# Cross attention in seven-product form on one core: half of the values' partition-group moves go from ScalarE to VectorE, and the values' sums stand ahead of the first transfer for x

## The chip, the cores and the metric

One core of one Trainium2 chip runs the kernel. The time is device microseconds of one execution, and the figure for a kernel is the median of its runs. The profile comes from one further execution, whose span (first to last instruction) is a little shorter than its device time.

## The reference, cut to what matters

x and y (`ctx_2048`) have the shape (32, 256, 1024): 32 samples, 256 channels C, 1024 positions N. Everything is fp32.

```
x_q = einsum('oc,bcn->bno', w_qk, y)
x_k = einsum('oc,bcn->bon', w_qk, x)
x_v = einsum('oc,bcn->bon', w_v, x) + b_v[None, :, None]
energy = einsum('bnc,bcm->bnm', x_q, x_k)
attention = softmax(energy, axis=-1)
attention = attention / (1e-07 + attention.sum(axis=1, keepdims=True))
x_r = einsum('bcn,bnm->bcm', x_v, attention)
x_r = relu(einsum('oc,bcn->bon', w_t, x - x_r) + b_t[None, :, None])
return x + x_r
```

Each row of the attention is normalized over m, then each column over n. The output is x plus a ReLU of a projection of x minus the attended values.

## The kernel before, in words

The weights are folded once: keys use w_qk^T w_qk, values use w_t w_v. After that the kernel loops over 32 samples b. Every matrix product is done in a 2x2 block form with seven products instead of eight (class `Seven`, methods `p1` to `p7`), so operands need sums of blocks (tiles `xs`, `ys`, `gt`, `us`, `et`), and the outputs are combined from PSUM banks (`c11`, `c12`, `c21`, `c22`). ScalarE copies products 1 and 5 and a partial result `w` out of PSUM (`kept`; tiles named `ep1s`, `ep5s`, `ew` for the energy), because later products are accumulated onto the same banks: product 6 goes onto bank one only after `ep1s` is copied, product 7 onto it only after `ew`, product 3 onto bank two only after `ep5s`.

For a sample there are four families of products: the keys (`Keys`, PSUM tiles `pg`, 7 products), the values (`Values`, `pu`, 7), the energy (`Energy`, `pe`, four row pairs t = 0 to 3, 28 products) and the attention with its projection (`Attention`, `po`, 35 products: 7 of x, 28 of the attention). That is 77 products of 128x128 by 128x512 for each sample. The trace records each as two MATMUL instructions.

The stages overlap by hand. The engines' instructions are issued in the order of the program (wrapper `InOrder`), and every engine works through its own queue in that order. The keys and values of sample b+1 and the first products of its energy are put among the energy and attention products of sample b. The loop over t runs the energy: `p1`, `p5`, `p6`, `p2`, `p3`, `p7` for t = 0; for later t, `p4` of the row pair before stands between `p6` and `p3`. Each pair's exponentials are on ScalarE (`exp`), the combining reductions with a running minimum or maximum and the column sums (`share`) on VectorE. Afterwards `columns` and `inverse` normalize the columns, and `Attention.run` scales e (`normal`), forms the sums `et` (`mix`) and multiplies.

The part that is changed: the values of the next sample come out with channels on the partitions and are needed with positions on the partitions. `Values.turn` transposes 32x32 blocks on VectorE from `ut` into `turned` (four instructions of 128x512), and `Values.move` then carries the blocks from one group of 32 partitions to another, back into `ut`. There are sixteen moves of 32 partitions x 512 elements, one for each pair of source and target group. Before the change all sixteen are ScalarE copies, in three lots in the energy of sample b at t = 0 (lines 669 to 719): six ahead of `p1`, four behind `p5`, six at the end of t = 0. (For the first sample they are DMAs on SyncE's queue.) When they are done, GpSimd forms the four sums `us` of the values (`Values.factors`), which the attention of that sample needs.

`summed("x", b + 1)` issues two plain loads from SyncE's queue into `xs` and returns three accumulating transfers, which GpSimd's queue issues (`xsteps`): each one waits for the one before it to land. Before the change the first stands at the end of t = 0, ahead of the four `us` sums, and the other two at the ends of t = 2 and t = 3.

Of the kernel before, what the change touches and what calls it, by code (L numbers as in the profile page):

```python
# [16 lines left out]
def kernel(  # L17
# [30 lines left out]
    B, C, N = x.shape  # L48
# [33 lines left out]
    pe, dve, act, pool = (InOrder(g) for g in (nc.tensor, nc.vector, nc.scalar, nc.gpsimd))  # L82
# [6 lines left out]
    def load(tag, b, pieces=1):  # L89
        from_, p = (x, xp) if tag == "x" else (y, yp)  # L90
        to = p.tile([P, KC, N], F32, tag=tag, name=f"{tag}_{b}")
        from_ = from_[b].rearrange("(k p) n -> p k n", p=P)
        W = KC // pieces
        for j in range(pieces):
            nc.sync.dma_start(to[:, ts(j, W)], from_[:, ts(j, W)])
        loaded[tag, b] = to

    def quarters(from_):

        return from_.rearrange("(k p) (h n) -> p k h n", p=P, h=MH)  # L100

    def corners(from_):

        q = quarters(from_)[:, 0, 0, :]
        return bass.AP(
            tensor=q.tensor, offset=q.offset, ap=[q.ap[0], [P * N + MB, 2], q.ap[-1]]
        )

    def accumulate(into, from_):
        return pool.dma_start(into, from_, accum_op=ALU.add)  # L110
# [113 lines left out]
    def summed(tag, b):  # L224


        p = up if tag == "x" else one
        s = p.tile([P, 4, MB], F32, tag=f"{tag}s", name=f"{tag}s_{b}")
        t1, t3, t4, t2 = (s[:, j] for j in range(4))
        to = loaded[tag, b]  # L230
        b11, b12 = to[:, 0, ts(0, MB)], to[:, 0, ts(1, MB)]
        b21, b22 = to[:, 1, ts(0, MB)], to[:, 1, ts(1, MB)]
        if b == 0:
            pool.tensor_tensor(t1, b11, b12, ALU.add)
            pool.tensor_tensor(t2, b22, t1, ALU.add)
            pool.tensor_tensor(t3, b12, b22, ALU.add)
            pool.tensor_tensor(t4, b21, t2, ALU.add)
            steps = []
        else:
            from_ = (x if tag == "x" else y)[b]  # L240
            q = quarters(from_)
            nc.sync.dma_start(s[:, :2], q[:, 0, 1:2, :].to_broadcast([P, 2, MB]))
            nc.sync.dma_start(s[:, 2:], q[:, 1])
            steps = [
                lambda: accumulate(s[:, :2], corners(from_)),
                lambda: accumulate(s[:, 2:], s[:, 0:1].to_broadcast([P, 2, MB])),
                lambda: accumulate(t4, q[:, 1, 1]),
            ]
        return (b11, b21, b22, t4, t1, t2, t3), steps
# [345 lines left out]
    def columns(b):  # L595

        dve.tensor_reduce(
            parts[:, :, 0],
            acc.rearrange("p (j r) -> p j r", r=G32),
            AX.X,  # L600
            ALU.add,
            apply_transpose=True,
        )
# [5 lines left out]
    def inverse(b):  # L609


        sc = one.tile([P, NB, 1], F32, tag="sc", name=f"sc_{b}")
        s = sc[:, :, 0]
        for a in range(1, NG):
            moved(parts[:G32, :, a], parts[ts(a, G32), :, 0])
        dve.tensor_reduce(s[:G32], parts[:G32], AX.X, ALU.add)
        dve.reciprocal(s[:G32], s[:G32])
        moved(s[G32 : 2 * G32], s[:G32])
        moved(s[2 * G32 :], s[: 2 * G32])
        rc = one.tile([P, NB, G32], F32, tag="rc", name=f"rc_{b}")  # L620
        dve.transpose(rc.rearrange("p j r -> p (j r)"), sc.to_broadcast([P, NB, G32]))
        return rc.rearrange("p j r -> p (j r)")
# [25 lines left out]
    xn, xsteps = summed("x", 1)  # L648
    xsteps[0]()
    u = Values(0, xr)  # L650
# [11 lines left out]
    for b in range(B):  # L662
        more = b + 1 < B
        pair = []

        for t in range(HT):
            now = Energy(b, t, lhs, rhs)
            pair.append(now)
            if t == 0 and b > 0:
                u.move(6, act.copy)  # L670
            now.p1()
            if t > 0:
                pair[t - 1].exp(1)
            now.p5()
            if t == 0:
                if b == 0:
                    u.p4()
                    u.c21()
                    u.turn()
                    u.move(16, nc.sync.dma_start)  # L680
                    xsteps[1]()
                    xsteps[2]()
                else:
                    u.move(4, act.copy)
                if b > 0 and more:
                    before.end()
                    before.c21()
                    load("x", b + 1)
                e = ep.tile([P, NT, N], F32, tag="e", name=f"e_{b}")
                acc = one.tile([P, N], F32, tag="acc", name=f"acc_{b}")  # L690
                if before is not None:

                    pool.tensor_copy(behind, before.t4[:, HT - 1, :1])
                for step in gsteps:
                    step()
            if t > 1:
                pair[t - 2].share(0)
            if t == 0:
                now.p6()
            now.p2()  # L700
            now.c11()
            if t == 1:
                pair[0].scale(1)
            if t > 1:
                pair[t - 1].share(1)
            if t > 0:
                now.p6()
            if t == 1:
                act.activation(acc, e[:, HT, :], AF.Copy, scale=scales[HT])
            if t > 0:  # L710
                pair[t - 1].p4()
                pair[t - 1].c21()
                pair[t - 1].exp(0)
            now.p3()
            now.c12()
            now.p7()
            now.c22()
            if t == 0:
                u.move(6, act.copy)
                ur, usteps = u.factors()  # L720
                if more and b > 0:
                    xn, xsteps = summed("x", b + 1)
                    xsteps[0]()
                for step in usteps:
                    step()
            elif more and b > 0 and t > 1:
                xsteps[t - 1]()
        last = pair[-1]

        if more:  # L730
            g = Keys(b + 1, xn)
            g.p1()
        last.exp(1)
        if more:
            g.p5()
        else:
            before.xpart(before.one, 7, True)
        pair[2].share(0)
        last.p4()
        last.c21()  # L740
        last.share(1)
        if more:
            load("y", b + 1)
            rhs, ysteps = summed("y", b + 1)
            g.p6()
        else:
            before.epart(before.one, 7)
        last.exp(0)
        if more:
            g.p2()  # L750
            g.c11()
            g.p3()
        else:
            now = Attention(b, xr, ur)
            now.begin()
        last.share(0)
        columns(b)
        if more:
            g.p7()
            g.c12()  # L760
            g.c22()
            un = Values(b + 1, xn)
            un.p1()
            un.p5()
            un.p2()
            un.p6()
        else:
            before.c22()
        rc = inverse(b)
        if more:  # L770
            un.p3()
            g.p4()
            g.c21()
            un.p7()
            lhs, gsteps = g.factors()

        if more:
            now = Attention(b, xr, ur)
            now.begin()
            ysteps[0]()  # L780
            now.run(un)
            if b + 2 < B:
                now.xpart(now.one, 7, True)
                now.epart(now.one, 7)
                now.c22()
                now.put()
            now.put()
            ysteps[1]()
            ysteps[2]()
            before = now  # L790
            xr, u = xn, un
        else:
            before.end()
            now.run(None, before)
            now.finish()
# [30 lines left out]
```

## Time and profile before

| | us |
|---|---|
| median of three runs | 2181.16 (2179.96 to 2182.82) |
| the profiled execution's device time | 2179.43 |
| its span | 2177.7 |
| PE busy in it | 2145.1 (99%) |
| DVE (VectorE) busy | 1793.1 (82%) |
| ACT (ScalarE) busy | 1096.0 (50%) |
| POOL (GpSimd) busy | 540.0 (25%) |
| granted TensorE clock | 0.998 |

Starts are microseconds from the start of the span. A line of the timeline gives start, length, engine, operation, target and source tile, shapes and how many instructions are merged into it, and in brackets how long the engine was idle before it and who ended that. Successive matmuls and successive VectorE instructions overlap at their ends, so the pitch from start to start is shorter than the length shown. Nearly all instructions carry line 77, which is the line of the recording wrapper; tiles tell them apart.

### The profile page before, as it was taken

The numbers are of one execution on the slowest core, as the hardware profiler recorded it, in microseconds if no ns is written. First come the engines' busy times: TensorE is split into PE (matmuls) and PEld (weight loads), VectorE is DVE, ScalarE is ACT, GpSimd is POOL, SyncE is SP. The second block draws the span as 40 slices with busy tenths as digits, with TensorE's granted clock in tenths as the row PEclk, the third lists the DMA queues.
The fourth block names the chain that finished last, engine by engine and source line by source line (L and its number), as shares of the span: only waits on it lengthen the run. The fifth ranks groups of instructions, "written<-read, shape, count | busy, mean of one in ns | idle before, by whom it ended". The sixth has DMA issues, their size and how long they took to land.

```text
span 2177.7 us, 17656 instructions
## 1 busy us (share of the span) xinstructions
PE 2145.1 (99%) x4972; PEld 933.7 (43%) x4972; DVE 1793.1 (82%) x3247; ACT 1096.0 (50%) x1818; POOL 540.0 (25%) x487
## 2 busy tenths in 40 slices
PE   9999999999999999999999999999999999999989
PEld 5444444444444444444444444444444444444433
DVE  6889778897778987788977889778897778987778
ACT  5444564445554455544455444564445654355542
POOL 4312222222222122221222312222222222222220
PEclk9999999999999999999999999999999999999999
DMA  6444544435444454444444444544435444354420
GB/s 174 102 107 110 135 126 106 121 92 140 122 112 125 95 127 130 121 111 106 116 128 133 102 104 113 135 126 107 117 96 140 122 108 128 92 130 128 119 54 29
DMA packets 114210, 249.94 MB, mean 115 GB/s; under 512 B 17088, under 2 KB 17856, under 8 KB 114112
## 3 DMA queue, kind: packets, MB, share of 16 engines
q0 software_dynamic: 42656, 81.28, 23.1%
q1 hardware_dynamic: 71456, 167.53, 21.9%
q8 instruction: 40, 0.66, 0.1%
q14 instruction: 58, 0.48, 0.1%
HBM read 181.67 MB, written 33.55 MB: 99 GB/s over the span
## 4 chain that ended last, share of the span: by engine, by line
PE 69%; ACT 17%; DVE 11%; issue 2%; ACTq 0%; DVEq 0%
PE po L77 27%; PE pe L77 24%; ACT ut L77 14%; PE pg L77 9%; PE pu L77 9%; DVE et L77 4%; DVE turned L77 3%; DVE e L77 1%; DVE z L77 1%; ACT z L77 1%; ACT ep1s L77 1%; ACT ep5s L77 1%; ACT ew L77 1%; DVE acc L77 0%; PE idle L77 0%
## 5 line engine op out<-in xcount | busy, mean ns | idle before, releaser
L77 PE MATMUL pe<-gt,ys 128*128 128x512 f32 x768 | 398.7, 601 | 26.4 <-ACT ep1s L77 18.8
L77 ACT COPY ut<-turned 32x512 f32<-32x512 f32 x496 | 305.3, 615 | 164.5 <-DVE turned L77 158.3
L77 DVE SCALAR_TENSOR_TENSOR e<-e,ri,rc 128x512 f32<-128x512 f32 x512 | 347.4, 747 | 1.1
L77 PE MATMUL po<-et,us 128*128 128x512 f32 x768 | 347.5, 594 | 0.7 <-DVE et L77 0.7
L77 DVE SCALAR_TENSOR_TENSOR acc<-e,ri,acc 128x1024 f32<-128x1024 f32 x224 | 288.3, 1287 | 8.0
L77 PE MATMUL pe<-gx,y 128*128 128x512 f32 x512 | 261.9, 593 | 0.0
L77 PEld LDWEIGHTS pe<-gt,ys 128*128 128x128 f32 x768 | 141.0, 190 | 230.9 <-issue 178.6
L77 PE MATMUL po<-e,ut 128*128 128x512 f32 x512 | 224.9, 592 | 0.0
L77 PEld LDWEIGHTS po<-et,us 128*128 128x128 f32 x768 | 143.2, 190 | 189.4 <-issue 145.8
L77 ACT ACTIVATE e<-e,nm 128x1024 f32<-128x1024 f32 x128 | 146.9, 1148 | 97.0 <-DVE nm L77 96.1
L77 POOL TENSOR_TENSOR gt<-gx 128x512 f32<-128x512 f32 x64 | 80.9, 1264 | 433.7 <-DVE gx L77 433.7
L77 DVE TENSOR_TENSOR z<-z,x 128x512 f32<-128x512 f32 x31 | 21.5, 692 | 182.8 <-ACT z L77 182.8
L77 POOL DMA_DIRECT2D xs<-in_x_dram x62 | 65.8, 1061 | 363.2 <-PE pe L77 225.9
L77 DVE TENSOR_TENSOR et<-e 128x1024 f32<-128x1024 f32 x128 | 153.7, 1222 | 2.3
L77 DVE CUSTOM_DVE_ANT_0 e<-pe,ep1s 128x512 f32<-128x512 f32 x128 | 88.2, 689 | 79.4 <-ACT ep1s L77 57.4
L77 PEld LDWEIGHTS pe<-gx,y 128*128 128x128 f32 x512 | 97.6, 191 | 123.0 <-issue 122.5
L77 PEld LDWEIGHTS po<-e,ut 128*128 128x128 f32 x512 | 97.3, 190 | 122.5 <-issue 99.0
L77 ACT ACTIVATE e<-e,bias 128x1024 f32<-128x1024 f32 x128 | 147.4, 1151 | 1.4 <-DVE bias L77 0.5
L77 PE MATMUL pe<-gt,y 128*128 128x512 f32 x256 | 131.3, 595 | 0.0
L77 PE MATMUL pe<-gx,ys 128*128 128x512 f32 x256 | 130.8, 592 | 0.2 <-DVE nm L77 0.2
L77 ACT ACTIVATE op5s<-po,bt 128x512 f32<-128x512 f32 x32 | 22.0, 687 | 200.5 <-PE po L77 200.5
L77 ACT ACTIVATE op1s<-po,bt 128x512 f32<-128x512 f32 x32 | 22.0, 687 | 197.7 <-PE po L77 197.7
(117 smaller groups left out, 3315.5 us busy)
## 6 DMA issues: line engine op xcount, KB each, us to landing
y<-in_ctx_dram SPq DMA_DIRECT2D x32, 1024.0 KB, 4.9
out_dram<-z SPq DMA_DIRECT2D x128, 256.0 KB, 2.1
x<-in_x_dram SPq DMA_DIRECT2D x31, 1024.0 KB, 7.5
xs<-in_x_dram SPq DMA_DIRECT2D x62, 512.0 KB, 4.6
ys<-in_ctx_dram SPq DMA_DIRECT2D x62, 512.0 KB, 4.5
xs<-in_x_dram POOLq DMA_DIRECT2D x31, 512.0 KB, 6.2
xs<-xs POOLq DMA_DIRECT2D x31, 512.0 KB, 5.0
ys<-in_ctx_dram POOLq DMA_DIRECT2D x31, 512.0 KB, 6.2
```

The source lines that it names most:

```text
L77: self.last = getattr(self.engine, name)(*args, **kwargs)
```

## The change

Of the sixteen moves of a sample, the first eight are now VectorE copies, issued right behind the last `put` of the sample before (for the last sample the first twelve). The remaining eight stay on ScalarE: five ahead of `p1` of t = 0 and three behind `p5`; the lot at the end of t = 0 is gone. For the last sample, ScalarE does four, at the end of t = 0, and none ahead of that. The four `us` sums on GpSimd now stand in t = 0 behind the sums of the keys (`gsteps`), and the three accumulating transfers for x come after them, at the ends of t = 1, 2 and 3. The two plain loads for `xs` keep their place in SyncE's queue.

```diff
             now = Energy(b, t, lhs, rhs)
             pair.append(now)
-            if t == 0 and b > 0:
-                u.move(6, act.copy)
+            if t == 0 and b > 0 and more:
+                u.move(5, act.copy)
             now.p1()
...
                     xsteps[1]()
                     xsteps[2]()
-                else:
-                    u.move(4, act.copy)
-                if b > 0 and more:
+                elif more:
+                    u.move(3, act.copy)
                     before.end()
                     before.c21()
                     load("x", b + 1)
...
                 for step in gsteps:
                     step()
+                if more:
+                    ur, usteps = u.factors()
+                    for step in usteps:
+                        step()
...
             now.c22()
-            if t == 0:
-                u.move(6, act.copy)
+            if t == 0 and not more:
+                u.move(4, act.copy)
                 ur, usteps = u.factors()
-                if more and b > 0:
-                    xn, xsteps = summed("x", b + 1)
-                    xsteps[0]()
                 for step in usteps:
                     step()
-            elif more and b > 0 and t > 1:
+            elif t == 0 and b > 0:
+                xn, xsteps = summed("x", b + 1)
+            elif more and b > 0:
                 xsteps[t - 1]()
...
             now.put()
+            un.move(8 if b + 2 < B else 12, dve.tensor_copy)
             ysteps[1]()
             ysteps[2]()
```

The prediction calls a product by its number and row pair: "p6 of t = 1" is the sixth product of the energy's second row pair.

## The prediction

> **What bounds the kernel now.** First the page's busy times. TensorE is busy for 2145.1 of 2177.7 us, VectorE for 82% of them; no other engine is near.
>
> ```profile
> PE 2145.1 (99%) x4972; PEld 933.7 (43%) x4972; DVE 1793.1 (82%) x3247; ACT 1096.0 (50%) x1818; POOL 540.0 (25%) x487
> ```
>
> So the question is how far TensorE is from running without a gap. In the PE timeline, fifteen undisturbed products from 638.47 to 651.35 give a pitch of 12.88 / 15 = 0.859 us. A sample has 77 products, 66.1 us. Samples start (p1 of t = 0) at 622.72, 690.01, 757.30: 67.29 us. TensorE loses 1.17 us a sample, about 35 us over the kernel, and that is all there is to gain between the two ends. The PE timeline shows where they lie:
>
> ```profile
> 630.44 1.02 PE L77 MATMUL pe<-gt,y 128*128 128x512 f32 x2
> 631.49 1.10 PE L77 MATMUL pe<-gt,ys 128*128 128x512 f32 x2
> 632.42 1.02 PE L77 MATMUL pe<-gx,y 128*128 128x512 f32 x2
> ...
> 634.14 1.02 PE L77 MATMUL pe<-gx,y 128*128 128x512 f32 x2
> 635.77 1.12 PE L77 MATMUL pe<-gt,ys 128*128 128x512 f32 x2 [0.61 <-ACT ep1s L77]
> 636.73 1.02 PE L77 MATMUL pe<-gx,ys 128*128 128x512 f32 x2
> ```
>
> Read start to start against 0.86. The line at 631.49 is p7 of t = 0 and comes 1.05 after its neighbour, 0.19 late; the next is 0.07 late. The line at 635.77 is p6 of t = 1 and comes 1.63 after its neighbour, 0.77 late, the next 0.10. Together 1.13 us. Another 0.04 is in the attention, where a product waits for the second half of an `et` sum. These lines return in every sample from 1 to 30 within 0.02 us.
>
> Who makes them late is in the ACT timeline:
>
> ```profile
> 622.78 3.76 ACT L77 COPY ut<-turned 32x512 f32<-32x512 f32 x6 [5.12 <-DVE turned L77]
> ...
> 627.66 2.50 ACT L77 COPY ut<-turned 32x512 f32<-32x512 f32 x4
> 630.18 0.69 ACT L77 ACTIVATE z<-po,bt 128x512 f32<-128x512 f32 x1
> 630.76 0.58 ACT L77 COPY ew<-pe 128x512 f32<-128x512 f32 x1
> 631.37 3.74 ACT L77 COPY ut<-turned 32x512 f32<-32x512 f32 x6
> 635.13 0.58 ACT L77 COPY ep1s<-pe 128x512 f32<-128x512 f32 x1
> ```
>
> ScalarE works through sixteen moves at 0.625 us with no idle time from 622.78 on. `ew` ends at 631.34 and holds p7; `ep1s` of t = 1 ends at 635.71 and holds p6, though its product (p1, 632.42) was through at 633.4.
>
> At the same time VectorE has nothing to do:
>
> ```profile
> 623.52 1.28 DVE L77 SCALAR_TENSOR_TENSOR z<-z,x 128x512 f32<-128x512 f32 x2
> 630.90 0.69 DVE L77 TENSOR_TENSOR z<-z,x 128x512 f32<-128x512 f32 x1 [6.09 <-ACT z L77]
> 631.51 0.68 DVE L77 CUSTOM_DVE_ANT_0 e<-pe,ep1s 128x512 f32<-128x512 f32 x1
> ```
>
> The moves go into that idle stretch of 6.09 us, 624.8 to 630.9.
>
> **The change part by part.**
>
> *ScalarE.* Eight moves go: 8 x 0.625 = 5.0 us. Its queue becomes: five moves from 622.78 to 625.90, `ep1s` and `ep5s` of t = 0 to 627.0, three moves to 628.9. The last attention product ends at 628.9, so `z` runs from 628.95 to 629.6. p6 of t = 0 ends at 629.74 (its start 628.72 plus 1.02), so `ew` runs from 629.8 to 630.4: p7, which TensorE could take at 631.30, no longer waits. Then ScalarE stands idle until p1 of t = 1 is through at about 633.2, `ep1s` is done at 633.8, and p6 is due at 634.73: 0.9 us to spare. All four late products go, the 0.07 and 0.10 with them, since they only follow an interrupted stream.
>
> *VectorE.* Eight copies of 32x512 are added. No copy of that kind is in the trace of before. The nearest rows of VectorE at 512 elements a partition are these:
>
> ```profile
> L77 DVE TENSOR_TENSOR z<-z,x 128x512 f32<-128x512 f32 x31 | 21.5, 692 | 182.8 <-ACT z L77 182.8
> L77 DVE MEMSET zeros<- 128x512 f32 x1 | 0.5, 485 | 0.1
> ```
>
> By the two-input row a move costs 0.69 us, eight 5.5, ending at 630.3. The Trainium skill ("VectorE: DVE Perf Modes", the perf-mode tier table) says that an fp32 copy inside SBUF runs at two elements a cycle, where a tensor_tensor has only one: by it and its 0.96 GHz, 256 cycles fewer than the row, 0.69 - 0.27 = 0.42 us (an estimate), and eight 3.4. I take 0.43, near the single-source memset row, and keep 0.42 to 0.69. The choice hardly matters in samples 1 to 30, as both ends lie under the cover of 6.09 us. What is queued behind the moves: the `z` addition (now possible at 629.7), then `c11`, `c12`, `c22` and `bias` of t = 0. Counting back from p3 of t = 1, due at 636.45: it needs `ep5s`, which stands behind the first exponential (1.15) on ScalarE, which needs `bias`; so `c22` must start by 633.75, and the moves must end by about 631.7. That is 6.9 us for eight, 0.86 each.
>
> *GpSimd and the transfers.* The four `us` sums (1.27 us each) start when the last move is done, about 629.0, and end at about 634.1; before, 635.2 to 640.3. The first accumulating transfer for x moves from 629.75 to about 634.1, the second from 640.22 to about 642.4, the third from 645.52 to about 648.5 (8.3 and 6.1 us from issue to next issue, as at 24.29, 32.57 and 38.71 in the first sample). Their readers are the next keys: product 5 at 652.2, product 6 at 653.9, product 4 at 661.6, each some 1.1 us earlier after the change. The second lands at about 649, four microseconds ahead of product 6; the third, at 4.0 us to landing plus about 1 of issue, at about 653.5, seven ahead of product 4. Cost nothing; if that cover were gone, lateness would hit TensorE directly. The plain loads on SyncE keep their place, so no other transfer is passed.
>
> A rule that speaks against this: the Trainium skill ("SBUF — State Buffer", "Who interferes with whom") says that a VectorE copy using both ports locks GpSimd out for its whole length, descriptor writing included. The trace shows such contention: in sample 0 the `us` sums take 2.25 us instead of 1.27 while VectorE's column sums beside them take up to 1.51 instead of 1.28. By the rule a transfer issued at 629.75 could still have met the moves. In the new order GpSimd's queue holds only the `us` sums there, and these wait for the moves anyway; its sums of the keys end at 622.4, before the moves. What remains is the `z` addition beside the first `us` sum: at most one length of that, 1.27 us, of the 2 us and more to spare. So nothing by either.
>
> *Samples 1 to 30:* 30 x 1.13 = 33.9 us.
>
> *The last sample.* Before, TensorE stood still for 7 us: p6 of t = 0 waited for `ep1s` behind the six leading moves.
>
> ```profile
> 2108.22 2.04 PE L77 MATMUL pe<-gt,ys 128*128 128x512 f32 x2 [6.94 <-issue]
> 2110.05 1.52 PE L77 MATMUL pe<-gx,y 128*128 128x512 f32 x2
> ```
>
> Now ScalarE copies at once, TensorE runs on through p6 of t = 1 to about 2108, and then p4 of t = 0 waits for VectorE, whose twelve moves begin at 2104.2. At 0.43 they end at 2109.4; `c11`, `c12`, `c22` and `bias` take 2.3, the exponential 1.25, `ep5s` 0.6: p3 of t = 1 at about 2113.6 instead of 2117.99. Gain 4.4, less some 0.7 for TensorE's slow restart (the two lines above, after 6.9 us of idling, are 1.5 slower than usual; the new pause is half as long): 3.7. At 0.69 a move it is 0.6.
>
> *Sum:* 37.6 us. The profiled execution's 2179.43 becomes 2141.8. The median of the runs lies 1.7 above that execution: 2143.5 us.
>
> **The rivals.**
>
> *VectorE takes over as the limit (0.17).* From `c11` of t = 2 (642.21) it has no idle time until the transposes, 45 us later, and at 674.5 a product takes an `et` half that ended 0.1 us before (the 0.04). If that stretch starts only part of 1.13 us earlier, the rest comes back there. For it: TensorE's weight loads wait for `et` two times a sample, 28.7 us in all. Against: `c11` of t = 2 followed its own product (641.04 + 1.02) after 0.25 us of idling, and the steps ahead of it also end on TensorE, so the stretch should move along whole. A loss of 0.3 to 0.5 a sample gives 2152 to 2158.
>
> *Transfers for x arrive late (0.03).* The new places cost them 2 to 4 us of slack. Two microseconds too late for product 6 would cost 30 x 2 = 60 and turn the result into a loss, 2204; it needs 6 us more than the first sample's spacing.
>
> *A VectorE move is dear (0.04).* Sixteen separate runs of 32 elements, from one partition group to another, could cost far more than a plain row. Beyond 0.86 us each, every further 0.1 costs 0.8 a sample; at 1.0 the gain of 1.13 is used up, at 1.1 the loss is about 0.8 x 30 plus 4 at the end, 2209. Against: no row of 512 elements costs over 0.75, and ScalarE's moves of that shape cost 615 ns against 586 for its plain copies.
>
> *The waits don't go (0.01).* Were ScalarE still late after eight moves less, the time would stay near 2180; it would need 0.9 us more.
>
> **How the numbers follow.** The forecast itself has 0.75: 2139.5 (moves at 0.4, the 0.04 gone too) to 2148. The range of 2139.5 to 2157 takes in most of VectorE's rival. A measurement here tells about 0.2%, 4.4 us, from no change. Faster: 0.75 + 0.17 and a little of the late transfers, 0.92. Same: 0.02. Slower: 0.06.
>
> **What would show it.** Right: a sample's period of 66.1 to 66.2 us; no `ep1s` among the PE waits; VectorE's copies of `ut` between about 624.8 and 629 in this sample's place, at 0.4 to 0.7 each; VectorE's idle time ahead of `z` mostly gone; accumulating transfers issued after the `us` sums, with GpSimd's `xs` chain done before the keys. Wrong: a new PE wait on `et`, on `nm` or on `xs` in each sample; copies above 0.86; a period above 66.5.

## The result, and the profile after

The changed kernel takes 2143.01 us in the median of six runs (2142.41 to 2144.14). The kernel before, in the same rounds, takes 2181.18 (2179.96 to 2182.82). The ratio is 0.9824, with a 95% interval of 0.9812 to 0.9837: 38.2 us faster. The profiled execution has a span of 2140.6 us, 37.1 less than before, at a granted clock of 0.999.

The busy times after the change, and the engines' shares of the chain of work that ended last, first after and then before:

```profile
PE 2130.6 (100%) x4972; PEld 941.3 (44%) x4972; DVE 1907.8 (89%) x3499; ACT 944.2 (44%) x1566; POOL 549.8 (26%) x487
...
PE 97%; DVE 3%; issue 0%; ACT 0%; DVEq 0%
```
```profile
PE 69%; ACT 17%; DVE 11%; issue 2%; ACTq 0%; DVEq 0%
```

VectorE gained 115 us of work and ScalarE lost 152, yet the span went down, and the chain runs through TensorE for 97% of the time. Before, 17% of that chain was ScalarE's.

The PE timeline, in the place that answers to the one shown of before (this sample starts at 615.03):

```profile
622.76 1.02 PE L77 MATMUL pe<-gt,y 128*128 128x512 f32 x2
623.62 1.02 PE L77 MATMUL pe<-gt,ys 128*128 128x512 f32 x2
624.48 1.02 PE L77 MATMUL pe<-gx,y 128*128 128x512 f32 x2
...
626.19 1.02 PE L77 MATMUL pe<-gx,y 128*128 128x512 f32 x2
627.05 1.02 PE L77 MATMUL pe<-gt,ys 128*128 128x512 f32 x2
627.91 1.02 PE L77 MATMUL pe<-gx,ys 128*128 128x512 f32 x2
```

Every pitch is 0.86. p7 of t = 0 (623.62) and p6 of t = 1 (627.05) come on time, and so do the products behind them. Samples start at 615.03, 681.16 and 747.30: the period is 66.13 us instead of 67.29, against 66.1 for 77 products without a gap. The list of what TensorE waited for (total, times, longest) has no `ep1s` any more; before (the first line), that was its largest entry:

```profile
PE pe L77 <- ACT ep1s L77: 18.8, 31, 0.6
```
```profile
PE pe L77 <- DVE nm L77: 3.5, 2, 3.3
PE po L77 <- DVE et L77: 1.1, 2, 0.5
PE idle L77 <- DVE few L77: 1.1, 1, 1.1
```

The ACT timeline shows why:

```profile
615.09 3.12 ACT L77 COPY ut<-turned 32x512 f32<-32x512 f32 x5 [5.12 <-DVE turned L77]
...
622.10 0.59 ACT L77 COPY ew<-pe 128x512 f32<-128x512 f32 x1 [0.17 <-PE pe L77]
...
625.53 0.59 ACT L77 COPY ep1s<-pe 128x512 f32<-128x512 f32 x1 [2.85 <-PE pe L77]
```

`ew` of t = 0 (622.10) and `ep1s` of t = 1 (625.53) now find ScalarE idle (0.17 and 2.85 us, ended by PE): they wait for their products, not for moves.

The DVE timeline has the moves, and the `z` addition behind them:

```profile
617.04 3.43 DVE L77 COPY ut<-turned 32x512 f32<-32x512 f32 x8
...
621.96 1.00 DVE L77 TENSOR_TENSOR z<-z,x 128x512 f32<-128x512 f32 x1 [1.49 <-ACT z L77]
```

Eight moves take 3.43 us, 0.428 each. The idle stretch ahead of `z` shrank from 6.09 to 1.49 us, and `z` itself grew from 0.69 to 1.00 because a `us` sum of GpSimd runs beside it:

```profile
621.14 1.27 POOL L77 TENSOR_TENSOR us<-ut 128x512 f32<-128x512 f32 x1 [6.42 <-ACT ut L77]
622.49 1.60 POOL L77 TENSOR_TENSOR us<-us,ut 128x512 f32<-128x512 f32 x1
626.49 1.20 POOL L77 DMA_DIRECT2D xs<-in_x_dram  x1
```

The second `us` sum takes 1.60 instead of 1.27. The first accumulating transfer for x goes out behind the last of them, at 626.49, the others at 632.95 and 638.26, and no product waits for them.

In the last sample TensorE now runs through p6 of t = 1, the first of these lines, and then stops for `nm`:

```profile
2073.75 1.02 PE L77 MATMUL pe<-gt,ys 128*128 128x512 f32 x2
2078.08 1.82 PE L77 MATMUL pe<-gx,ys 128*128 128x512 f32 x2 [3.31 <-DVE nm L77]
2080.01 1.99 PE L77 MATMUL pe<-gt,y 128*128 128x512 f32 x2
```

The two products behind the stop take 1.93 and 1.83 us to the next start instead of 0.86; the granted clock of 2078 to 2082 is 0.57.

### The profile page after: what moved, and what is told of

Read it like the earlier page. It is cut to its first block, busy times and chain, and to the rows that moved or that the text cites. A ratio compares the mean times of both kernels' runs of the same rounds, so it can differ in the third digit from the quotient of the medians.

```text
span 2140.6 us, 17690 instructions
## 1 busy us (share of the span) xinstructions
PE 2130.6 (100%) x4972; PEld 941.3 (44%) x4972; DVE 1907.8 (89%) x3499; ACT 944.2 (44%) x1566; POOL 549.8 (26%) x487
## 4 chain that ended last, share of the span: by engine, by line
PE 97%; DVE 3%; issue 0%; ACT 0%; DVEq 0%
PE po L77 43%; PE pe L77 35%; PE pg L77 9%; PE pu L77 9%; DVE e L77 1%; DVE acc L77 0%; DVE et L77 0%; DVE ut L77 0%; PE idle L77 0%; DVE z L77 0%; DVE rc L77 0%; DVE parts L77 0%; DVE turned L77 0%; DVE sc L77 0%; DVE gx L77 0%
## 5 line engine op out<-in xcount | busy, mean ns | idle before, releaser
L77 PE MATMUL pe<-gt,ys 128*128 128x512 f32 x768 | 392.1, 592 | 0.0
L77 PEld LDWEIGHTS pe<-gt,ys 128*128 128x128 f32 x768 | 146.0, 190 | 184.4 <-issue 182.6
L77 ACT COPY ut<-turned 32x512 f32<-32x512 f32 x244 | 150.0, 615 | 157.4 <-DVE turned L77 154.6
L77 DVE CUSTOM_DVE_ANT_0 e<-pe,ep1s 128x512 f32<-128x512 f32 x128 | 88.5, 691 | 64.1 <-ACT e L77 63.1
L77 POOL TENSOR_TENSOR us<-ut 128x512 f32<-128x512 f32 x64 | 82.0, 1282 | 206.2 <-ACT ut L77 192.4
L77 ACT COPY ep1s<-pe 128x512 f32<-128x512 f32 x128 | 74.5, 582 | 114.5 <-PE pe L77 107.2
L77 PE MATMUL po<-e,us 128*128 128x512 f32 x256 | 120.5, 592 | 0.0
L77 DVE CUSTOM_DVE_ANT_0 e<-pe,zeros,nm 128x512 f32<-128x512 f32 x128 | 95.7, 748 | 27.3 <-PE pe L77 26.1
```

The costliest lines, as they stand in the source:

```text
L77: self.last = getattr(self.engine, name)(*args, **kwargs)
```

## The experiments

The theory: all of the gain comes from taking eight moves off ScalarE, as VectorE had an idle stretch that ends only with the attention's last product. The rivals: the new order on GpSimd does part of it; VectorE is close to being the limit, so the moves cost something; the first product to be late sets the size, so fewer or more moves would be better. Ratios are to the kernel before, with 95% intervals.

### The two parts of the change, each alone

VectorE's moves, with GpSimd's order as before (the first lines taken out stand behind the sums of the keys):

```diff
-                if more:
-                    ur, usteps = u.factors()
-                    for step in usteps:
-                        step()
...
-            if t == 0 and not more:
-                u.move(4, act.copy)
+            if t == 0:
+                if not more:
+                    u.move(4, act.copy)
                 ur, usteps = u.factors()
+                if more and b > 0:
+                    xn, xsteps = summed("x", b + 1)
+                    xsteps[0]()
                 for step in usteps:
                     step()
-            elif t == 0 and b > 0:
-                xn, xsteps = summed("x", b + 1)
-            elif more and b > 0:
+            elif more and b > 0 and t > 1:
                 xsteps[t - 1]()
```

> The moves as in the changed kernel (8 on VectorE, 5 + 3 on ScalarE), but GpSimd's queue in the old order: first x transfer ahead of the us sums at the end of t = 0, the others at the ends of t = 2 and 3. Theory (ScalarE's backlog was the whole stall, GpSimd's order is worth nothing): period 66.13 us a sample, time 2143 within 4 us. Rival (the new order of GpSimd's queue brought part of the gain, by the port that it shares with VectorE or by slack for the transfers): period above 66.3, time 2150 or more, if half the gain is its own 2162.

Measured: 2142.29 us, ratio 0.9826 (0.9811 to 0.984), period 66.13. So GpSimd's order is worth nothing to the time. The `z` addition takes 0.69 here instead of 1.00, since the sums start later, and that is worth nothing either.

The converse, the kernel before with GpSimd's new order and all moves on ScalarE:

```diff
             if t == 0:
                 u.move(6, act.copy)
                 ur, usteps = u.factors()
-                if more and b > 0:
-                    xn, xsteps = summed("x", b + 1)
-                    xsteps[0]()
                 for step in usteps:
                     step()
-            elif more and b > 0 and t > 1:
+                if more and b > 0:
+                    xn, xsteps = summed("x", b + 1)
+            elif more and b > 0:
                 xsteps[t - 1]()
```

> The kernel before, with all sixteen moves on ScalarE in lots of 6, 4 and 6, and only GpSimd's queue changed: us sums first, then the three x transfers at the ends of t = 1, 2 and 3. Theory: period 67.29, time 2181 within 4 us, the 0.77 ahead of p6 of t = 1 still there. Rival (GpSimd's order matters): faster by 10 us or more, 2171 or less.

Measured: 2180.73 us, ratio 0.9999 (0.9989 to 1.0008), period 67.28. In its PE timeline the stop of the kernel before is still there:

```profile
636.60 1.12 PE L77 MATMUL pe<-gt,ys 128*128 128x512 f32 x2 [0.62 <-ACT ep1s L77]
```

The two parts add up: nothing and all.

### How many moves on VectorE

Six instead of eight, with ten on ScalarE; for sixteen, ScalarE's two lots are 0 and VectorE's is 16:

```diff
-                u.move(5, act.copy)
+                u.move(6, act.copy)
...
-                    u.move(3, act.copy)
+                    u.move(4, act.copy)
...
-            un.move(8 if b + 2 < B else 12, dve.tensor_copy)
+            un.move(6 if b + 2 < B else 12, dve.tensor_copy)
```

> Six moves on VectorE, ten on ScalarE in lots of 6 and 4 (the first two lots of the kernel before), no third lot. Theory: ScalarE is done with ew at about 631.4 in the time of before, so p7 of t = 0 is still 0.19 late and the next product 0.07, but the 0.77 and 0.10 at p6 of t = 1 are gone: period 66.13 + 0.26 = 66.39, time 2143 + 30 x 0.26 = 2151. Rival (every move taken from ScalarE counts its 0.625 us until the stall is used up): the stalls fall by the same amount whichever lot goes, six moves are 3.75 us against 1.13, so 2143.

Six measured 2150.13 us, 0.986 (0.9845 to 0.9874), period 66.38. p7 of t = 0 is 0.17 late and the next product 0.07, and p6 of t = 1 is on time. That isolates the smaller of the two losses: with ten moves ahead of it on ScalarE, `ew` starts at 623.78 and holds p7, whatever happens at the end of t = 0.

> All sixteen moves of samples 2 to 31 on VectorE, none on ScalarE (the last sample as in the changed kernel). They take 16 x 0.428 = 6.85 us and end 31.65 - 24.8 = 6.85 us after the last put, where the prediction set the latest harmless end at 6.9. Theory: 0 to 0.3 us a sample lost, 2143 to 2152, and the first place to go late is p3 of t = 1 behind ep5s. Rival (VectorE is at its limit as soon as its idle stretch of 6.09 us is full): 0.76 us over it is lost in every sample, 2143 + 23 = 2166.

Sixteen measured 2146.02 us, 0.9841 (0.9825 to 0.9858), period 66.22. The moves run from 618.23 for 6.89 us, almost exactly the 6.9 that the prediction gave as the latest harmless end. `ep5s` of t = 1 is ready at 629.90, p3 of t = 1 starts at 629.96, just in time, and the product behind it comes 0.09 late. So the limit is where the count backwards put it.

Twenty, of which four copy blocks that were already moved (ScalarE's two lots are 0, as with sixteen):

```diff
-            un.move(8 if b + 2 < B else 12, dve.tensor_copy)
+            un.move(16 if b + 2 < B else 12, dve.tensor_copy)
+            if b + 2 < B:
+                un.moves = [(a, g) for a in range(NG) for g in range(NG)][:4]
+                un.move(4, dve.tensor_copy)
```

> As with sixteen moves on VectorE, and the first four of them are carried out a second time there (the same data to the same place): twenty copies, 20 x 0.428 = 8.6 us. With sixteen, p3 of t = 1 was 0.09 late, so there is no slack left. Theory: each further copy costs its whole 0.43, 1.71 us a sample: period 66.22 + 1.71 = 67.93, time 2146 + 29 x 1.7 = 2196, slower than before by 0.7%. Rival (VectorE's load only counts by its share of the span, 92% with twenty copies, so it still has room): at most 0.3 us a sample, 2155 or less.

Measured: 2202.36 us, 1.0095 (1.0081 to 1.0109), period 68.09. This kernel is slower than before. The DVE and the PE timeline of one sample:

```profile
631.36 8.75 DVE L77 COPY ut<-turned 32x512 f32<-32x512 f32 x20
```
```profile
643.01 1.13 PE L77 MATMUL pe<-gx,ys 128*128 128x512 f32 x2 [0.62 <-DVE nm L77]
644.95 1.12 PE L77 MATMUL pe<-gt,y 128*128 128x512 f32 x2 [0.81 <-ACT ep5s L77]
```

The moves are 1.86 us longer than with sixteen, and the period is 1.87 longer. The losses are 0.78 at p4 of t = 0 (waiting for VectorE's `nm`), 1.07 at p3 of t = 1 (for `ep5s`, behind the exponential) and 0.10 behind it. The expectation was 0.16 a sample too low, because the four further copies lengthen the moves by 1.86 and not by 1.71: the first four and the last four start 0.45 apart instead of 0.43. Past the limit the stretch is paid one for one. The chain from the moves to p3 of t = 1 is the one that the prediction named, and by the same count eight moves at twice their cost, 6.9 us, would have left a gain as well.

### Is VectorE at its limit in the stretch of 45 us?

The rival of the prediction with 0.17 said that VectorE has no slack there. One more memset of 512 elements a partition is put into the stretch, ahead of the column sums (the first line added), and in a second kernel behind the moves instead (the second one):

```diff
+        dve.memset(zeros, 0.0)
...
             un.move(8 if b + 2 < B else 12, dve.tensor_copy)
+            dve.memset(zeros, 0.0)
```

> The changed kernel with one more VectorE instruction in each sample, a rewrite of the zeros tile (128x512, 0.42 to 0.49 us), ahead of the column sums, inside the stretch where VectorE has no idle time. Theory (VectorE is just in time at the et sums, so its next bound is this stretch): nearly all of it comes out in the period, 66.13 + 0.4 = 66.5, time 2143 + 31 x 0.4 = 2155. Rival (VectorE still has slack, 89% busy): nothing, 2143.

> The same instruction directly behind the moves, in what is left of VectorE's idle stretch (1.5 us). Theory: hidden in samples 1 to 30 and 0.4 us at the last sample, 2143.5, period 66.13. Rival (any VectorE time counts): as in the stretch, 2155.

In the stretch: 2154.67 us, 0.9881 (0.9866 to 0.9895), period 66.49. Behind the moves: 2144.5 us, 0.9832 (0.9817 to 0.9846), period 66.13. The memset takes 0.49 alone. The eight products of `et` with `us`, as merged in the two PE timelines:

```profile
600.52 3.99 PE L77 MATMUL po<-et,us 128*128 128x512 f32 x8
```
```profile
597.81 3.64 PE L77 MATMUL po<-et,us 128*128 128x512 f32 x8
```

The first is of the kernel with the memset in the stretch, the second of the one with it behind the moves. The extra 0.35 sits inside one group of products, the one that loses 0.04 after the change. The same instruction is free in one place and costs 0.36 a sample in the other (66.49 less 66.13). VectorE thus has almost no slack for `et`, as the rival feared (0.49 put in, 0.36 lost, so about 0.1 to spare), but the moves lie ahead of the point where the stretch is set by a product, so they never touched it. The rival described the resource rightly and the change wrongly.

### The last sample

Its twelve early moves on VectorE, taken back to 6, 4 and 6 on ScalarE:

```diff
-            if t == 0 and b > 0 and more:
-                u.move(5, act.copy)
+            if t == 0 and b > 0:
+                u.move(5 if more else 6, act.copy)
...
-            un.move(8 if b + 2 < B else 12, dve.tensor_copy)
+            if b + 2 < B:
+                un.move(8, dve.tensor_copy)
```

> The changed kernel with only the last sample as before: its sixteen moves on ScalarE in lots of 6, 4 and 6. Theory: the period stays 66.13 and the last sample loses the 3.6 us again: 2146.6. Rival (the last sample gains nothing of its own, the difference between the two tails is only the one period of sample 30): 2143.

Measured: 2146.43 us, 0.984 (0.9827 to 0.9853). The last sample's part of the gain is 3.4 us by the medians. The stop of 6.94 us is back in the PE timeline, with three products at double pitch behind it.

Eight on VectorE and eight on ScalarE:

```diff
-                u.move(4, act.copy)
+                u.move(8, act.copy)
...
-            un.move(8 if b + 2 < B else 12, dve.tensor_copy)
+            un.move(8, dve.tensor_copy)
```

> The changed kernel, but the last sample has eight moves on VectorE and eight on ScalarE instead of twelve and four. Theory (in the last sample VectorE's moves hold p4 of t = 0): four copies less are 1.7 us, and ScalarE is done with its eight before the first exponential is due: tail 1.7 shorter, 2141.3. Rival (the time from the last sample's start to the end is set by the long VectorE work behind it, and the moves hide beside other waits): 2143.

Measured: 2140.56 us, 0.981 (0.9797 to 0.9824). The stop is now at p6 of t = 1 and shorter:

```profile
2076.14 1.19 PE L77 MATMUL pe<-gt,ys 128*128 128x512 f32 x2 [1.98 <-ACT ep1s L77]
2077.12 1.91 PE L77 MATMUL pe<-gx,ys 128*128 128x512 f32 x2
2078.82 1.85 PE L77 MATMUL pe<-gt,y 128*128 128x512 f32 x2
```

The clock fell nevertheless: granted 0.51 from 2077 to 2080.5, two products at double pitch.

No VectorE moves in the last sample; ScalarE spreads them over the ends of the row pairs, and nine follow the last exponential, with the `us` sums behind them:

```diff
-            if t == 0 and not more:
-                u.move(4, act.copy)
-                ur, usteps = u.factors()
-                for step in usteps:
-                    step()
+            if not more:
+                u.move((3, 1, 1, 1)[t], act.copy)
...
         last.exp(1)
+        if not more:
+            u.move(1, act.copy)
...
         last.exp(0)
+        if not more:
+            u.move(9, act.copy)
+            ur, usteps = u.factors()
+            for step in usteps:
+                step()
...
-            un.move(8 if b + 2 < B else 12, dve.tensor_copy)
+            if b + 2 < B:
+                un.move(8, dve.tensor_copy)
```

> The changed kernel, but the last sample has no move on VectorE and none ahead of its energy: three ScalarE moves at the end of t = 0, one at the end of each later t, one behind the last exponential of the upper half and nine behind the very last one, and the us sums after these. Theory: nothing holds the energy products of the last sample any more (3.47 us of waiting and about 2.0 of slow restart go), ScalarE and GpSimd are idle in the stretch where VectorE normalizes, so moves and sums hide there: 4 to 5.5 us less, 2137.5 to 2139. Rival (the attention's first products come 9 us after the last exponential and now wait for the nine moves, 5.6 us, and the sums, 5.1): gain under 2, 2141 to 2143.

Measured: 2139.22 us (2138.36 to 2140.09), 0.9807 (0.9794 to 0.9821), just above the expected 2137.5 to 2139. The energy of the last sample no longer stops for moves, but the attention now has stops:

```profile
2102.08 1.12 PE L77 MATMUL po<-e,ut 128*128 128x512 f32 x2 [0.43 <-DVE e L77]
...
2110.85 1.96 PE L77 MATMUL po<-et,us 128*128 128x512 f32 x4 [0.87 <-DVE et L77]
```

VectorE's ten scalings (`normal`) are late. They take 10.04 us here and 6.72 in the kernel with the old last sample:

```profile
2099.30 10.04 DVE L77 SCALAR_TENSOR_TENSOR e<-e,ri,rc 128x512 f32<-128x512 f32 x10
```
```profile
2109.19 6.72 DVE L77 SCALAR_TENSOR_TENSOR e<-e,ri,rc 128x512 f32<-128x512 f32 x10
```

The four `us` sums run beside them, from 2098.54 to 2104.8. Taken one by one in the trace, the first four scalings last 1.05, 1.75, 1.75 and 1.75, the other six 0.74, and the last two sums 1.71 instead of 1.26. Each of the four scalings starts while a sum runs, and each of the last three sums while a scaling runs: they take turns, one scaling to one sum. To show that these are the cause, four of the nine late moves go into ScalarE's gaps ahead of two exponentials, which ends the sums earlier:

```diff
                 pair[t - 1].c21()
+                if not more and t > 1:
+                    u.move(2, act.copy)
                 pair[t - 1].exp(0)
...
         if not more:
-            u.move(9, act.copy)
+            u.move(5, act.copy)
```

> As in the run with the last sample's moves on ScalarE behind the chain (2139.22 us), but four of the nine moves behind the last exponential go into ScalarE's idle gaps of 1.47 and 1.43 us ahead of the exponentials of t = 1 and t = 2 in rows t = 2 and t = 3. The moves then end about 2.5 us earlier (2096.0 instead of 2098.5), and the us sums run from about 2096.0 to 2101.3, so they meet VectorE's ten normal scalings (from 2099.3) for 2 us instead of 5.5. Theory (the scalings took 10.04 us instead of 6.72 because the us sums ran beside them, 0.6 us for each us beside): scalings about 7.9 us, the TensorE waits on e mostly gone, about 2.1 us less than that run, 2137.1 us. Rival (the scalings are long for another reason, such as the order of their inputs in the new queue): 10 us again and 2139.2. A second rival: the gaps are not free, p7 of t = 2 or t = 3 waits for ew, or the exponentials come late; then a new TensorE wait of up to 1 us shows in the energy, and 2138 to 2140.

Measured: 2138.47 us (2137.99 to 2139.1), 0.9804 (0.9791 to 0.9818). The sums run from 2097.36 to 2102.9 and the scalings start at 2100.61:

```profile
2100.61 8.09 DVE L77 SCALAR_TENSOR_TENSOR e<-e,ri,rc 128x512 f32<-128x512 f32 x10
```

8.09, where 7.9 was expected: 1.37 us extra for 2.25 us side by side, against 3.32 for 5.5 in the run before; 0.6 a microsecond both times. So the sums are the cause. From the start of the last sample to the end of the span it is 70.6 us against 72.6, the 2 us that were expected. The medians differ by 0.75 only, their ranges overlap, and this one is 1.4 above the expected 2137.1. In the profiled execution of this kernel the first product of the energy came 1.4 us later (22.14 against 20.78), and such an offset at the start differs from execution to execution; that it also accounts for the medians is not shown.

This is the version that points beyond the change: 2138.47 us is 4.5 below it by the medians, at about the bound of 0.2% that the prediction set, and the trace shows where it comes from.

### A transfer issued beside the moves

The prediction weighed a rule by which VectorE's copies lock out GpSimd's descriptor writing. After the change no transfer is issued beside them. With sixteen moves on VectorE, as in the diff, and GpSimd's order of the first experiment, one is:

```diff
-                u.move(5, act.copy)
+                u.move(0, act.copy)
...
-                    u.move(3, act.copy)
+                    u.move(0, act.copy)
...
-            un.move(8 if b + 2 < B else 12, dve.tensor_copy)
+            un.move(16 if b + 2 < B else 12, dve.tensor_copy)
```

> All sixteen moves on VectorE, and GpSimd's queue in the old order, so that the first x transfer is issued while VectorE copies (moves from about 618 to 625 in the sample at 616, plain loads landed at about 622.6). Theory by the shared port as the Trainium skill has it: the issue lasts until a copy lets it in, longer than its usual 1.2 us, up to the end of the moves; the transfer is later by that, which its slack covers, so the time is that of sixteen moves with the new order, 2146 within 4. Rival (no lock for this kind of copy): the issue lasts 1.2 us and time is 2146 as well; only the length of the issue tells.

Measured: 2146.68 us, 0.9844 (0.9828 to 0.9861), the same as sixteen with the new order (2146.02). The DVE and the POOL timeline:

```profile
618.20 6.89 DVE L77 COPY ut<-turned 32x512 f32<-32x512 f32 x16
```
```profile
623.19 1.22 POOL L77 DMA_DIRECT2D xs<-in_x_dram  x1 [7.32 <-DMA xs<-in_x_dram]
```

The issue lies inside the copies and takes 1.22 us, as it does where VectorE is idle (1.22 at 629.75 in the kernel before). The median landing of its group is 6.2 us, as in the kernel before. The copies are not slower either (6.89 for sixteen in both). The lock is seen neither in the length of the issue nor in the landing. The DMA packets in the trace agree: the transfer's first packet starts 1.92 us behind the start of the issue, against 1.95 in the kernel before, though the copies end only 1.90 behind it; in 28 of thirty samples it starts 1.91 to 2.00 us behind. When the descriptors are written the trace does not show.

## Why the prediction was right

2143.5 us was predicted and 2143.01 measured, the mechanism is the one that was named, and the terms of the sum hold to about 1 us each. That they agree to half a microsecond is partly luck: samples 1 to 31 brought 38.5 and not 37.6, the start of the profiled execution took 1.4 back, and the median of the runs lies 0.6 above that execution where 1.7 was taken.

- *Samples 1 to 30.* 33.9 us predicted: 1.13 from each of thirty. The 29 periods between the starts of samples 1 and 30 show 33.8, and sample 30 brings 1.2 more, 35.0 in all. Of a loss of 1.17 a sample the prediction itemised 1.13 and kept 0.04; 1.16 came back, so the term is 1.1 us short.
- *The move.* 0.43 taken, 0.428 measured. The Trainium skill ("VectorE: DVE Perf Modes", the perf-mode tier table) put it far below the two-input row of 0.69, and its rule is the one that the trace bears out, with 0.42 by the prediction's estimate, even for 16 runs of 32 elements that change their partition group.
- *The cover.* Ten moves on ScalarE still hold p7; sixteen on VectorE end at the latest harmless point; twenty are a loss. The limit of 6.9 us was right to a tenth.
- *The `z` addition beside a `us` sum.* At most 1.27 predicted, 0.3 on either engine measured, hidden as said. The Trainium skill ("SBUF — State Buffer", "Who interferes with whom") says of this pair, a VectorE instruction with two SBUF inputs and a GpSimd instruction that reads SBUF, that they contend. The trace agrees: `z` goes from 692 to 984 ns in the mean. In the sample shown it starts when the first sum has 0.45 us left, and loses 0.30; the second sum starts when `z` has 0.47 left, and loses 0.33.
- *The transfers.* Predicted 11.4, 19.7 and 25.8 us behind the sample's start (634.1, 642.4 and 648.5 less 622.72); measured 11.5, 17.9 and 23.2. The spacing of the first sample was too careful. Nothing waits for them.
- *The last sample.* 4.4 less 0.7 predicted, 3.7. By the PE timelines, p3 of t = 1 starts 14.13 us behind the sample's start (2065.88) instead of 18.59 (2099.40), a gain of 4.46; the product behind it starts after 15.96 instead of 19.47, so 0.95 goes to the slow restart and 3.5 is left. The size of the restart was nearly right, though not its reason: it does not shrink with the pause. All slow products together cost 2.04 behind the stop of 3.31 us, and 1.47 behind the one of 6.94 before.
- *What was not predicted.* Sample 1 starts at 85.79 instead of 84.35 in the profiled execution. 0.72 of the 1.44 is already there at the first product of the energy (21.96 against 21.24), and over the profiled executions of this study that product starts anywhere from 20.71 to 22.18. The other 0.7 is in sample 0, and the kernel with GpSimd's new order alone, whose sample 0 is the same as before, has it too (21.43 to 85.24, 63.8 instead of 63.1). So nothing shows that the change is its cause. It hid the 1 us by which the first term was short.

Of the rivals, only "VectorE takes over as the limit" had substance: that stretch has 0.1 us to spare, and the change simply does not add to it.

## What to carry to other kernels

Look for the engine that stands idle in the very window in which another one makes the critical engine late, and count backwards from the next product that needs it: the latest harmless end (here 6.9 us for the moves) says how much work fits, and it was right on both sides of the limit. An engine that is busy for 89% can take more work ahead of a point where it waits anyway, and hardly any in the stretch behind it; the same half microsecond cost nothing in one place and 0.36 a sample in the other. GpSimd's sums put beside VectorE's two-input instructions are not free even if GpSimd is idle, so move them under single-input ones: in the last experiment on the last sample, the three sums that run beside VectorE's reductions and its transpose take their usual 1.26.

## What the runs showed of the hardware

- The price of a stop of TensorE is not in proportion to it. Stops of 0.4 to 0.9 us cost about 0.1 beyond themselves. The 1.98 us stop cost 1.8 more: the granted clock was 0.51 for about 3.4 us (2077.12 to 2080.51), and this began one product behind the stop. The 3.31 us stop cost 2.04, the 6.94 us stop 1.47 in one kernel and 2.8 in another with the same stop.
- Of a VectorE instruction with two SBUF inputs and a `us` sum on GpSimd, the one that starts second loses nearly all that the other still has to run. After the change `z` lost 0.30 of 0.45 us and the next sum 0.33 of 0.47; with the late moves in the last sample, a scaling lost 1.01 of 1.20 and the sum behind it 0.45 of 0.59. The one that starts first loses nothing: the first sum that `z` meets after the change takes 1.27, and with sixteen moves and GpSimd's old order, where `z` starts first, `z` takes 0.69 and the sum 1.70. The 0.6 us lost for each microsecond side by side is the mean of such turns.
- In the first experiment the first accumulating transfer has a median landing of 9.4 us instead of 6.2 to 6.3 in all the other kernels. There the first `us` sum starts 0.78 us behind the start of the issue, elsewhere at least 2 us behind it or ahead of the transfer, and its packets start at about half the rate that they have in the kernel before. No product waited for it, and no run tests whether the sums are the cause.
